# First pair with its adjacency chunks loaded ahead of x, most of its operands built on Pool, and each later pair's scale spread to all partitions by two DMAs

## The chip, the cores and the metric

The kernel runs on one core of one Trainium2 chip. The time is device microseconds of that core, the median of three runs. TensorE multiplies, VectorE and ScalarE (ACT) work on elements, Pool (GpSimd) and SyncE (SP) issue most of the transfers; SP's and ACT's transfers are generated by hardware, Pool's by software.

## The reference

```
def _L0_gnn_ref(cur, incidence_m):              # N = 4096, D = 512
    mask = incidence_m > 0
    head = mask.astype(incidence_m.dtype)
    head = head / maximum(sqrt(sum(head * head, axis=-1)), EPS)
    inc = incidence_m + head
    return (inc @ cur) / sum(inc, axis=-1)

def _L1_gnn_ref(X, A, W):
    A2 = A + eye(N)
    dscale = diagonal(A2) ** (-0.5)
    temp = A2 @ X @ W.T
    return relu((dscale[:, None] * A2 * dscale[None, :]) @ temp)

x = layernorm(x + _L0_gnn_ref(x, adj))
x = layernorm(x + _L1_gnn_ref(x, adj, W))
```

All is fp32; adj is 4096 x 4096. Each row of `inc` is adj plus, at its positive entries, one over the square root of their number. That number per row is what the text calls the scale (its reciprocal root).

## The kernel before, in words

The big products are done by a Strassen-like scheme with seven products in place of eight. Layer 0 works on 16 pairs of row blocks (rows j x 128 and (j + 16) x 128). A pair goes through four chunks; a chunk `a` holds 128 partitions by four quarters by 512 columns of the transposed adjacency, 1 MB, loaded by SP into a ring of three. For every chunk VectorE (`prepare1`)

- adds two quarters into `sr` (line 383), the raw sums that a Pool DMA (line 403) writes to `oa` in DRAM for layer 1;
- makes the mask times scale by one product for each half (393) and adds it to the chunk (395);
- forms four sums `s` (`add_up`, lines 159 to 162).

TensorE (`multiply1`, 417) then multiplies the four 128-column parts with blocks of x, seven products each, into seven PSUM banks: 28 products, 56 matmul instructions. The x side of these products needs four sums too, T1 to T4; `build` makes them once for each of the 16 blocks on VectorE (123 to 126), four instructions of 128x256. After four chunks `combine` empties the banks, and `layer0` and `operands` finish the previous pair during the next.

The scale of a pair must lie along the free dimension and be equal on all partitions. For pair 0, `count_first` takes signs of the four chunks on ACT (302), and 32 matmuls with a matrix of ones add them up over partitions and leave the total in all partitions (320). For later pairs ACT counts the signs of 16 tiles `nat` of the natural adjacency, and `spread` has three parts: reduce and root (355, 306 to 308); reciprocal and two diagonal matrices `d` (360, 363); a matmul of ones with `d` (368) and a copy out of PSUM (370). In steady state parts 0, 1 and 2 stand at chunk 2 of a pair around `prepare1` and `multiply1`; for pair 1 they stand at chunk 3 of pair 0.

The order is written out by hand: each engine takes its instructions in program order, and waits on semaphores only for what it reads or overwrites. SP issues in order, with at most eight transfers under way, each on one of eight semaphores in turn. At the start SP loads four blocks of x, three chunks and the fourth chunk (`last`, which is loaded again later), then the rest of x with five `nat` tiles in between. VectorE builds blocks 0 to 3 first, the other twelve during the chunks of pair 0.

After layer 0, layer 1's products (lines 252 and 625) fill the time from about 830 us on; nothing there is changed.

Of the kernel before, what the change touches and what calls it, by code (L numbers as in the profile page):

```python
# [8 lines left out]
F32 = mybir.dt.float32  # L9
BF16 = mybir.dt.bfloat16  # L10
AF = mybir.ActivationFunctionType
ALU = mybir.AluOpType

P = 128
LN_EPS = 1e-5
EPS = 1e-12


A12, A11, A22, A21 = range(4)

B11, B21, B22, T1, T2, T3, T4 = range(7)
# [5 lines left out]
def tile_adj_resnorm_d2(  # L27
# [37 lines left out]
    nc = tc.nc  # L65
    N, D = x.shape
    H = D // 2
    NB = N // P
    NP = NB // 2
    ND = D // P  # L70
    CK = 4
    NC = NP // CK
    CW = CK * P
    W = H + 2
# [20 lines left out]
    def spare():  # L95
        return bank(7)
# [8 lines left out]
    nc.gpsimd.memset(eps_t, LN_EPS)  # L105
    tiny = const.tile([P, 1], F32, name="tiny")
    nc.gpsimd.memset(tiny, -(2.0 ** -63))
    dscale = const.tile([P, NB], F32, name="dscale")
    nc.gpsimd.dma_start(out=dscale, in_=diag)

# [10 lines left out]
    def outer_sums(t, b11, b12, b21, b22):  # L121

        nc.vector.tensor_sub(t[:, 0, :], b11, b12)
        nc.vector.tensor_sub(t[:, 2, :], b22, b12)
        nc.vector.scalar_tensor_tensor(t[:, 1, :], t[:, 0, :], -1.0, b22, op0=ALU.mult, op1=ALU.subtract)
        nc.vector.tensor_add(t[:, 3, :], b21, t[:, 1, :])

# [139 lines left out]
    w1_pool = scope.enter_context(tc.tile_pool(name="w1", bufs=2))  # L267
    pools["turn"], pools["work"] = [ring] * 2, work

    ones_f = w1_pool.tile([P, P], F32, name="ones_f", bufs=1)  # L270
    nc.gpsimd.memset(ones_f, 1.0)
    ones_b = w1_pool.tile([P, P], BF16, name="ones_b", bufs=1)
    nc.gpsimd.memset(ones_b, 1.0)
    chunks, sums, slots, counts, scale, natural = {}, {}, {}, {}, {}, {}
    xr = {}

    def half_tile(dtype=F32, width=CW):
        return w1_pool.tile([P, 2, width], dtype, tag="u", name="u", bufs=3)

    def load_chunk(n):  # L280
        a = ring.tile([P, 4, CW], F32, tag="a", name="a")
# [2 lines left out]

    def load_x(kk):

        s = feats_pool.tile([P, 7, W], F32, name=f"b{kk}")
        lo, hi = x[kk * P:(kk + 1) * P, :], x[(kk + NP) * P:(kk + NP + 1) * P, :]
        nc.sync.dma_start(out=s[:, B11:T4 + 1:T4, 0:H], in_=split(lo))
        nc.sync.dma_start(out=s[:, B21:B22 + 1, 0:H], in_=split(hi))  # L290
        nc.gpsimd.memset(s[:, B11:B21 + 1, H:W], 1.0)
        nc.gpsimd.memset(s[:, T1, H:W], 1.0)
        slots[kk] = s

    def build(kk):

        s = slots[kk]
        outer_sums(s[:, T1:T4 + 1, 0:H], s[:, B11, 0:H], s[:, T4, 0:H], s[:, B21, 0:H], s[:, B22, 0:H])

    def signs(y, a, accum=None):  # L300

        nc.scalar.activation(y, a, AF.Sign, bias=tiny, scale=2.0 ** 64, accum_out=accum)  # L302

    def to_scale(n, total):

        nc.vector.tensor_scalar(n, total, 0.5, N / 2, op0=ALU.mult, op1=ALU.add)
        nc.vector.tensor_scalar(n, n, EPS * EPS, None, op0=ALU.max)
        nc.scalar.activation(n, n, AF.Sqrt)

    def count_first(parts):  # L310

        ps = spare()[:, 0:2 * P].rearrange("p (h i) -> p h i", h=2)
        for c, a in enumerate(parts):
            m = half_tile(BF16, 2 * CW)
            m = m.rearrange("p h (q i) -> p (h q) i", q=2)
            signs(m, a)
            for i in range(CK):
                for z in range(2):
                    first, last = c + i + z == 0, c == NC - 1 and i == CK - 1 and z == 1
                    nc.tensor.matmul(ps, ones_b, m[:, z::2, i * P:(i + 1) * P], start=first, stop=last)  # L320
        s = w1_pool.tile([P, 2, P], F32, name="sc")
        to_scale(s, ps)
        nc.vector.reciprocal(s, s)
        scale[0] = s

    tiles = iter([(j, h, t) for j in range(1, NP) for h in range(2) for t in range(NT)])
    waiting = []
# [18 lines left out]
            signs(nat, nat, counts[j][:, h, t:t + 1])  # L346
            load_natural()

    spreading = {}

    def spread(j, part):

        if part == 0:
            n = small.tile([P, 2], F32, name="n")
            nc.vector.tensor_reduce(n, counts.pop(j), axis=mybir.AxisListType.X, op=ALU.add)
            to_scale(n, n)
            spreading[j] = n
        elif part == 1:
            n = spreading.pop(j)
            nc.vector.reciprocal(n, n)  # L360
            d = w1_pool.tile([P, 2, P], F32, name="d", bufs=1)
            for h in range(2):
                nc.vector.tensor_scalar(d[:, h, :], ident, n[:, h:h + 1], None, op0=ALU.mult)
            spreading[j] = d
        else:
            d = spreading.pop(j)
            ps = spare()
            nc.tensor.matmul(ps[:, 0:2 * P], ones_f, d.rearrange("p h i -> p (h i)"), start=True, stop=True)  # L368
            s = w1_pool.tile([P, 2, P], F32, name="sc")
            nc.scalar.copy(s.rearrange("p h i -> p (h i)"), ps[:, 0:2 * P])  # L370
            scale[j] = s

    def prepare1(n, pieces=1):


        j, c = divmod(n, NC)
        a, s = chunks[n], scale[j]
        sr, *masks = (half_tile() for _ in range(3))
        sums[n] = work.tile([P, 4, CW], F32, tag="s", name="s")
        for i in range(pieces):  # L380
            w = CW // pieces
            cols = slice(i * w, (i + 1) * w)
            nc.vector.tensor_add(sr[:, :, cols], a[:, A11:A22 + 1, cols],  # L383
                                 a[:, A21, cols].unsqueeze(1).to_broadcast([P, 2, w]))
            for h in range(2):
                t = masks[h]
                y, z = t[:, :, cols], a[:, 2 * h:2 * h + 2, cols]
                if pieces == 1:
                    parts = [[v.rearrange("p q (b i) -> p (q b) i", i=P) for v in (y, z)]]
                else:  # L390
                    parts = [[v[:, q, :].rearrange("p (b i) -> p b i", i=P) for v in (y, z)] for q in range(2)]
                for m, v in parts:
                    nc.vector.scalar_tensor_tensor(m, v, 0.0, s[:, h, :].unsqueeze(1).to_broadcast(list(v.shape)),  # L393
                                                   op0=ALU.is_gt, op1=ALU.mult)
                nc.vector.tensor_add(a[:, 2 * h:2 * h + 2, cols], a[:, 2 * h:2 * h + 2, cols], t[:, :, cols])  # L395
            add_up(sums[n][:, :, cols], a[:, :, cols])
        if j // CK == c:
            add_identity(sr[:, :, (j % CK) * P:(j % CK + 1) * P])

        q = ((A11, A12), (A21, A22))[j // NQ][c * CK // NQ]  # L400
        i0 = j % SB * P
        dst = outer_1[j % NQ // SB][c % (NQ // CK), :, :, q, i0:i0 + P].rearrange("k p i -> p k i")
        nc.gpsimd.dma_start(out=dst, in_=sr.rearrange("p m (k i) -> p (m k) i", i=P))  # L403

    def multiply1(n, acc):
        c = n % NC
# [58 lines left out]
        nc.gpsimd.dma_start(out=in_outer(2, j, slice(T1, T4 + 1)), in_=t)  # L465


    for kk in range(CK):
        load_x(kk)
    for n in range(3):  # L470
        load_chunk(n)
    last = work.tile([P, 4, CW], F32, tag="s", name="s")
    nc.sync.dma_start(out=last, in_=adj_q[0, NC - 1])
    for kk in range(CK, NP):
        load_x(kk)
        if kk >= 2 * CK and len(waiting) < 5:
            load_natural()
    for kk in range(CK):
        build(kk)
    count_first([chunks[0], chunks[1], chunks[2], last])  # L480
    prepare1(0, pieces=CK)

    C = None
    for n in range(NP * NC):
        j, c = divmod(n, NC)
        if c == 0:
            if j > 0:
                C = combine(acc)
            acc = [bank(m) for m in range(7)]
        if n + 2 >= NP * NC:  # L490
            load_up_to(n + 2 - NP * NC)
        elif n > 0:
            load_chunk(n + 2)
        if j == 0 and c < NC - 1:
            for kk in range((c + 1) * CK, (c + 2) * CK):
                build(kk)
        if j + 1 < NP and c == (3 if j == 0 else 2):
            spread(j + 1, 0)
            if j == 0:
                spread(1, 1)  # L500
                spread(1, 2)
        if n + 1 < NP * NC:
            prepare1(n + 1)
        else:
            prepare(0)
        if 0 < j < NP - 1 and c == 2:
            spread(j + 1, 1)
        multiply1(n, acc)
        if 0 < j < NP - 1 and c == 2:
            spread(j + 1, 2)  # L510
        count(((5, 5, 6, 4) if j == 0 else (6, 6, 0, 4))[c])
        if j == 1 and c == 1:
            nc.vector.tensor_scalar(dscale, dscale, 1.0, None, op0=ALU.add)
            nc.scalar.activation(dscale, dscale, AF.Sqrt)
            nc.vector.reciprocal(dscale, dscale)
        if j > 0 and c == 1:
            layer0(j - 1, C)
        if j > 0 and c == 2:
            operands(j - 1, C)
        if c == 3:  # L520
            load_rows(j)
# [291 lines left out]
```

## Time and profile before

| | |
|---|---|
| median of 3 runs | 2347.87 us (2345.51 to 2349.18) |
| the profiled execution | 2345.41 us |
| its span | 2343.6 us |
| TensorE busy | 2277.4 us, 97% |
| VectorE busy | 1832.7 us, 78% |
| ACT, Pool busy | 351.5 and 220.7 us |
| moved by DMA | 552.97 MB, 236 GB/s on average |
| first product of pair 0 | at 28.10 us |

The profile is of one execution. Its page gives busy times, a chain of work followed back from the end, and groups of instructions by line; the trace behind it answers by stretch of time or by engine. "Idle before, releaser" is the time an engine stood still ahead of an instruction, and what it waited for. Matmul instructions are counted singly: an fp32 product is two of them.

### The profile page before, as it was taken

What the parts mean: (1) busy time and instruction counts of PE and PEld (TensorE: products, weight loads), DVE (VectorE), ACT (ScalarE), POOL (GpSimd) and SP (SyncE); (2) the same over time, 40 slices, a digit from 0 to 9 for tenths busy, and PEclk for the clock granted to TensorE, in tenths of its full rate; (3) what the DMA queues carried; (4) which work ended last, traced back from release to release, by engine and by line L of the source; (5) the groups of instructions that cost most, each with busy time, mean ns of one, the idle gap of its engine ahead of it and who ended that gap; (6) DMA issues with size and microseconds to landing.
All of it is one profiled execution on the core that took longest, in us unless ns stands there. A gap on an engine that the chain in (4) does not pass through costs nothing.

```text
span 2343.6 us, 21028 instructions
## 1 busy us (share of the span) xinstructions
PE 2277.4 (97%) x7166; PEld 1352.6 (58%) x7166; DVE 1832.7 (78%) x2727; ACT 351.5 (15%) x806; POOL 220.7 (9%) x372
## 2 busy tenths in 40 slices
PE   4999999999999999999999999999999999999996
PEld 3788888888888844444444444444444444444443
DVE  6898888888889857888666779766567798767796
ACT  3232333323333000000000000000000011200013
POOL 0011111111111110000001100011100000000010
PEclk8999999999999999999999999999999999999998
DMA  9577777777776466575566757567666576765672
GB/s 318 197 252 252 262 244 253 258 255 260 251 256 235 172 261 242 207 276 204 202 252 229 274 186 267 186 237 286 225 238 223 214 253 237 267 231 216 224 260 77
DMA packets 148011, 552.97 MB, mean 236 GB/s; under 512 B 15920, under 2 KB 24128, under 8 KB 108864
## 3 DMA queue, kind: packets, MB, share of 16 engines
q1 hardware_dynamic: 114192, 418.42, 51.0%
q0 software_dynamic: 33712, 133.21, 14.9%
q8 instruction: 57, 0.93, 0.2%
q14 instruction: 50, 0.41, 0.0%
HBM read 438.32 MB, written 113.25 MB: 235 GB/s over the span
## 4 chain that ended last, share of the span: by engine, by line
PE 86%; DVE 8%; issue 3%; DMA 2%; ACT 0%; POOL 0%; SPq 0%; ACTq 0%; DVEq 0%; POOLq 0%
PE q L252 55%; PE q L417 26%; PE q L625 5%; DVE a L395 1%; DVE u L393 1%; DVE s L159 1%; DMA a<-oa 1%; DVE u L383 1%; DMA s<-adj_q 1%; DVE s L161 1%; PE q L645 1%; DMA oa<-u 0%; DVE c L553 0%; DVE s L162 0%; PE q L368 0%
## 5 line engine op out<-in xcount | busy, mean ns | idle before, releaser
L252 PE MATMUL q<-s,ts 128*128 128x512 f32 x1344 | 616.0, 594 | 1.0 <-DVE u L544 1.0
L417 PE MATMUL q<-b,s 128*128 128x256 f32 (+1 forms) x2048 | 488.5, 381 | 2.3 <-DVE s L161 2.3
L159 DVE TENSOR_TENSOR s<-a 128x1024 f32<-128x1024 f32 (+1 forms) x243 | 294.1, 1210 | 203.5 <-PE q L252 173.8
L252 PEld LDWEIGHTS q<-s,ts 128*128 128x128 f32 x1344 | 256.2, 191 | 325.7 <-issue 296.6
L417 PEld LDWEIGHTS q<-b,s 128*128 128x128 f32 x2048 | 389.8, 190 | 61.0 <-DVE s L161 3.7
L417 PE MATMUL q<-b,a 128*128 128x258 f32 (+1 forms) x1536 | 381.8, 383 | 10.1 <-issue 10.1
L252 PE MATMUL q<-a,tr 128*128 128x512 f32 x704 | 333.5, 596 | 5.1 <-DMA tr<-ob 4.2
L417 PEld LDWEIGHTS q<-b,a 128*128 128x128 f32 x1536 | 293.9, 192 | 52.9 <-issue 10.7
L252 PE MATMUL q<-s,tr 128*128 128x512 f32 x448 | 228.8, 592 | 0.0
L252 PEld LDWEIGHTS q<-a,tr 128*128 128x128 f32 x704 | 132.1, 191 | 162.1 <-issue 158.1
L302 ACT ACTIVATE nat<-nat,tiny 128x512 f32<-128x512 f32 x240 | 171.0, 715 | 208.2 <-DMA nat<-adj 208.1
L252 PE MATMUL q<-a,ts 128*128 128x512 f32 x352 | 180.2, 593 | 3.1 <-DVE c L549 2.9
L393 DVE SCALAR_TENSOR_TENSOR u<-a,sc 128x1024 f32<-128x1024 f32 (+1 forms) x142 | 157.6, 1114 | 24.8 <-ACT sc L370 14.4
L161 DVE TENSOR_TENSOR s<-a,s 128x512 f32<-128x512 f32 (+1 forms) x243 | 166.5, 685 | 8.3
L162 DVE TENSOR_TENSOR s<-a,s 128x512 f32<-128x512 f32 (+1 forms) x243 | 166.5, 685 | 8.3
L395 DVE TENSOR_TENSOR a<-a,u 128x1024 f32<-128x1024 f32 (+1 forms) x134 | 157.7, 1177 | 6.8
L252 PEld LDWEIGHTS q<-s,tr 128*128 128x128 f32 x448 | 85.1, 190 | 107.3 <-issue 99.0
L542 ACT COPY p<-q 128x512 f32<-128x512 f32 x28 | 16.4, 585 | 754.9 <-PE q L252 754.9
L252 PEld LDWEIGHTS q<-a,ts 128*128 128x128 f32 x352 | 66.5, 190 | 88.7 <-issue 77.0
L625 PE MATMUL q<-wt,c 128*128 128x512 f32 x256 | 115.1, 592 | 0.0
L159 DVE TENSOR_TENSOR s<-r 128x1024 f32<-128x1024 f32 x48 | 58.7, 1223 | 70.1 <-PE q L252 65.0
L403 POOL DMA_DIRECT2D oa<-u x64 | 57.6, 901 | 465.8 <-DVE u L383 211.2
(121 smaller groups left out, 1581.2 us busy)
## 6 DMA issues: line engine op xcount, KB each, us to landing
a<-adj_r SPq DMA_DIRECT2D x112, 1024.0 KB, 6.1
a<-oa SPq DMA_DIRECT2D x80, 1024.0 KB, 5.3
a<-adj_q SPq DMA_DIRECT2D x64, 1024.0 KB, 6.1
nat<-adj SPq DMA_DIRECT2D x240, 256.0 KB, 6.9
tr<-ob SPq DMA_DIRECT2D x112, 512.0 KB, 3.7
oa<-u POOLq DMA_DIRECT2D x64, 512.0 KB, 7.9
oa<-r POOLq DMA_DIRECT2D x32, 1024.0 KB, 6.6
y<-x POOLq DMA_DIRECT2D x64, 256.0 KB, 6.1
```

The source lines that it names most:

```text
L159: nc.vector.tensor_add(s[:, S3:S1 + 1, :], a[:, A11:A22 + 1, :], a[:, A21, :].unsqueeze(1).to_broadcast([P, 2, w]))
L161: nc.vector.tensor_add(s[:, S2, :], a[:, A11, :], s[:, S1, :])
L162: nc.vector.tensor_add(s[:, S4, :], a[:, A12, :], s[:, S2, :])
L252: nc.tensor.matmul(acc[m], left, right, start=(kk == 0), stop=(kk == NQ - 1))
L302: nc.scalar.activation(y, a, AF.Sign, bias=tiny, scale=2.0 ** 64, accum_out=accum)
L383: nc.vector.tensor_add(sr[:, :, cols], a[:, A11:A22 + 1, cols], a[:, A21, cols].unsqueeze(1).to_broadcast([P, 2, w]))
L393: nc.vector.scalar_tensor_tensor(m, v, 0.0, s[:, h, :].unsqueeze(1).to_broadcast(list(v.shape)), op0=ALU.is_gt, op1=ALU.mult)
L395: nc.vector.tensor_add(a[:, 2 * h:2 * h + 2, cols], a[:, 2 * h:2 * h + 2, cols], t[:, :, cols])
L403: nc.gpsimd.dma_start(out=dst, in_=sr.rearrange("p m (k i) -> p (m k) i", i=P))
L417: nc.tensor.matmul(acc[m][:, 0:w], left, b[:, right, 0:w], start=(kk == 0), stop=(kk == NP - 1))
L625: nc.tensor.matmul(pv, C_of[2][h][f][:, 2 * r + e, cols], wt[:, 2 * f + e, :], start=(f + e == 0), stop=(f + e == 2))
L645: nc.tensor.transpose(ps[:, at + i * P:at + (i + 1) * P], C_of[3][h][d // 2][:, 2 * r + d % 2, cols], ident)
```

## The change

The diff has three parts.

- Order of the start: the four chunks of pair 0 are loaded ahead of x, and counted in halves as they land. The signs go into the places of blocks 12 to 15 of x, which are not loaded yet. The raw sums of chunks 0 and 1 (`raw_sums`, split from `prepare1`) are made early. A first Sqrt on a 128x1 tile stands ahead of all signs.
- Operands: `build` has another form (one 128x512 instruction and three of 128x256), and takes an engine: Pool for blocks 4 to 15, VectorE for 0 to 3, which stand between parts of chunk 0's work. Pool's builds stand behind the raw-sum DMAs of chunks 0 and 1 and ahead of those of chunks 2 and 3.
- Scale: half the sum plus N/2 is put into ACT's Sqrt as scale and bias, and the maximum comes after it. For pairs 1 to 15 the 128x2 result goes by a DMA on ACT's queue to DRAM, and by a second to a 128x128x2 tile in all partitions; the diagonals, the matmul, the copy and `ones_f` go. The scale tile now has its two halves interleaved, so the product reads it with a step of two elements. All pairs have the same place for this, chunk 2; counts in pair 0 move from 5, 5, 6, 4 to 8, 8, 0, 4.

The shared buffers `u` (three) become `mask` (one) and `sr` (two).

```diff
+    half_n = const.tile([P, 1], F32, name="half_n")
+    nc.gpsimd.memset(half_n, N / 2)
+    nc.scalar.activation(small.tile([P, 1], F32, name="sd"), eps_t, AF.Sqrt)
...
-    def build(kk):
-        s = slots[kk]
-        outer_sums(s[:, T1:T4 + 1, 0:H], s[:, B11, 0:H], s[:, T4, 0:H], s[:, B21, 0:H], s[:, B22, 0:H])
+    def build(kk, engine):
+        s = slots[kk][:, :, 0:H]
+        engine.tensor_sub(s[:, T1:T3 + 1:2, :], s[:, B11:B22 + 1:2, :],
+                          s[:, T4, :].unsqueeze(1).to_broadcast([P, 2, H]))
+        engine.tensor_sub(s[:, T2, :], s[:, T4, :], s[:, B11, :])
+        engine.tensor_sub(s[:, T2, :], s[:, T2, :], s[:, B22, :])
+        engine.tensor_add(s[:, T4, :], s[:, B21, :], s[:, T2, :])
...
     def to_scale(n, total):
-        nc.vector.tensor_scalar(n, total, 0.5, N / 2, op0=ALU.mult, op1=ALU.add)
-        nc.vector.tensor_scalar(n, n, EPS * EPS, None, op0=ALU.max)
-        nc.scalar.activation(n, n, AF.Sqrt)
+        nc.scalar.activation(n, total, AF.Sqrt, bias=half_n, scale=0.5)
...
     def spread(j, part):
         if part == 0:
...
-        elif part == 1:
-            n = spreading.pop(j)
-            nc.vector.reciprocal(n, n)
-            d = w1_pool.tile([P, 2, P], F32, name="d", bufs=1)
-            for h in range(2):
-                nc.vector.tensor_scalar(d[:, h, :], ident, n[:, h:h + 1], None, op0=ALU.mult)
-            spreading[j] = d
-        else:
-            d = spreading.pop(j)
-            ps = spare()
-            nc.tensor.matmul(ps[:, 0:2 * P], ones_f, d.rearrange("p h i -> p (h i)"), start=True, stop=True)
-            s = w1_pool.tile([P, 2, P], F32, name="sc")
-            nc.scalar.copy(s.rearrange("p h i -> p (h i)"), ps[:, 0:2 * P])
-            scale[j] = s
+        else:
+            n = scale.pop(j)
+            nc.vector.tensor_scalar(n, n, EPS, None, op0=ALU.max)
+            nc.vector.reciprocal(n, n)
+            row = dram.tile([P, 2], F32, name=f"sc{j}")
+            nc.scalar.dma_start(out=row, in_=n)
+            scale[j] = w1_pool.tile([P, P, 2], F32, name="sc")
+            nc.scalar.dma_start(out=scale[j].rearrange("p i h -> p (i h)"),
+                                in_=row.rearrange("i h -> (i h)").partition_broadcast(P))
...
-    for kk in range(CK):
-        load_x(kk)
-    for n in range(3):
+    for n in range(NC - 1):
         load_chunk(n)
     last = work.tile([P, 4, CW], F32, tag="s", name="s")
     nc.sync.dma_start(out=last, in_=adj_q[0, NC - 1])
+    for c in range(NC):
+        count_first(0, c, chunks[c] if c < NC - 1 else last, ps)
+    for kk in range(2 * CK):
+        load_x(kk)
+    while len(waiting) < 5:
+        load_natural()
+    for kk in range(2 * CK, NP):
+        load_x(kk)
+    for n in range(2):
+        early.add(n)
+        raw_sums(n)
     for kk in range(CK, NP):
-        load_x(kk)
-        if kk >= 2 * CK and len(waiting) < 5:
-            load_natural()
-    for kk in range(CK):
-        build(kk)
-    count_first([chunks[0], chunks[1], chunks[2], last])
-    prepare1(0, pieces=CK)
+        build(kk, nc.gpsimd)
+    build(0, nc.vector)
+    scale[0] = w1_pool.tile([P, P, 2], F32, name="sc")
+    to_scale(scale[0], ps)
+    nc.vector.tensor_scalar(scale[0], scale[0], EPS, None, op0=ALU.max)
+    nc.vector.reciprocal(scale[0], scale[0])
+    sums[0] = work.tile([P, 4, CW], F32, tag="s", name="s")
+    to_inc(0, slice(0, P))
+    build(1, nc.vector)
+    to_inc(0, slice(P, CW))
+    build(2, nc.vector)
+    build(3, nc.vector)
...
-        if j == 0 and c < NC - 1:
-            for kk in range((c + 1) * CK, (c + 2) * CK):
-                build(kk)
...
+        scales = j < NP - 1 and c == 2
+        if scales:
             spread(j + 1, 0)
...
-            prepare1(n + 1)
+            prepare1(n + 1, between=(lambda: spread(j + 1, 1)) if scales else None)
...
-        count(((5, 5, 6, 4) if j == 0 else (6, 6, 0, 4))[c])
+        count(((8, 8, 0, 4) if j == 0 else (6, 6, 0, 4))[c])
```

In the new `prepare1` the raw sums come first (unless made early), then `between` (maximum, reciprocal and the two DMAs of the next scale), then `to_inc` (mask products, additions and `add_up`), which for chunk 0 is called with columns 0 to 127 and 128 to 511.

## The prediction

> **What bounds the kernel now.** I read the page's busy times first.
>
> ```profile
> PE 2277.4 (97%) x7166; PEld 1352.6 (58%) x7166; DVE 1832.7 (78%) x2727; ACT 351.5 (15%) x806; POOL 220.7 (9%) x372
> ```
>
> TensorE is idle for only 66 us of 2343.6, so a gain must either remove TensorE work or fill idle time. Next, the answer by stages says where the idle time is (columns: stretch, its length, busy PE, PEld, DVE, ACT, POOL with counts, granted clock, DMA share, GB/s).
>
> ```profile
> 0.00:28.00 28.00, 5.80 (x32) 3.83 (x32) 9.57 (x24) 10.77 (x7) 2.94 (x43) 0.99 0.94 336
> 28.00:45.00 17.00, 15.39 (x56) 12.57 (x56) 16.24 (x52) 5.93 (x15) 0.91 (x1) 0.82 1.08 374
> 45.00:60.00 15.00, 8.41 (x23) 6.40 (x24) 14.66 (x26) 5.96 (x16) 0.89 (x1) 0.66 0.57 193
> 60.00:85.00 25.00, 19.75 (x91) 16.62 (x89) 23.93 (x40) 1.02 (x3) 1.77 (x2) 0.94 0.53 189
> ...
> 100.00:150.00 50.00, 50.00 (x232) 43.73 (x231) 44.68 (x70) 16.34 (x46) 7.85 (x11) 1.00 0.71 244
> ```
>
> Up to 85 us VectorE is nearly full (14.66 of 15, 23.93 of 25) while TensorE waits; from 100 us on TensorE is full and VectorE has some 5 us in 50 to spare. The waiting is in TensorE's own order of time (start, duration, line, what it writes and reads, then the idle time before it):
>
> ```profile
> 42.90 0.59 PE L417 MATMUL q<-b,a 128*128 128x256 f32 x2
> 49.32 2.06 PE L417 MATMUL q<-b,a 128*128 128x258 f32 x4 [5.82 <-issue]
> 53.65 3.79 PE L417 MATMUL q<-b,s 128*128 128x256 f32 x8 [2.27 <-DVE s L161]
> ...
> 85.02 1.22 PE L368 MATMUL q<-d,ones_f 128*128 128x256 f32 x2 [5.27 <-DVE d L363]
> ```
>
> The last fence is the chain of work that ended last. A pair is 224 matmul instructions in 48.53 us, so a chunk (56) takes 12.13, and the broadcast matmul L368 stands in the chain once a pair.
>
> ```profile
> 86.24 49.88 PE q L417 x224
> 136.12 0.43 PE q L368 x2
> 136.55 48.53 PE q L417 x224
> 185.09 0.43 PE q L368 x2
> ```
>
> The first pair's last chunk starts at 86.24, so the first chunk of pair 1 ends at 86.24 + 2 x 12.13 = 110.5. From there TensorE runs full. This is my reference point: what it moves by, the end moves by. The page's chain agrees: L417 26% and L252 55% of it are TensorE.
>
> **What the Trainium skill says.** (1) SBUF — State Buffer, "Who interferes with whom": a VectorE instruction with two SBUF inputs contends with a GpSimd instruction that reads SBUF; "the other fully blocks". The trace of before has no such overlap: after 4 us Pool only issues DMAs. (2) GPSIMD Engine Reference, "3.1 Elementwise — side-by-side cycle accounting": an fp32 two-input add of 2048 elements takes 4497 ns on GpSimd at about 2.6 cycles an element. Scaled, 512 elements are about 1.17 us and 256 about 0.62; estimates from that page, with no row here beside them (VectorE's 256-wide ones take 0.42). (3) SBUF — State Buffer, "Door 1", on 16-byte lines: two hits a line keep full rate. The scale is now read with a step of 8 bytes, just inside; no row of before has such a step.
>
> **The change part by part.**
>
> *Steady state, pairs 1 to 15.* L368 leaves TensorE: 0.43 us a pair. For 14 pairs (the one in the first pair is part of the head below) 14 x 0.43 = 6.0 us of pure gain, as TensorE is full there. VectorE loses L306, L307 and two L363 (0.17 + 0.17 + 0.48) and gains a maximum (0.17): 0.65 us lighter, from about 44.3 to 43.7 of 48.5. In place of the matmul, ACT issues a store of 1 KB and, when that has landed, a load to 128 partitions. Behind these on ACT are four counting activations; the copies that empty PSUM come some 24 us later, so they are covered. VectorE's sums of the raw chunk precede the maximum, so the scale is asked for at about 222.3 in the frame of the third pair (L383 at 220.88 plus 1.14 and two small ones) and first used at about 232.5 (L383 at 231.72, plus 1.14, less what is dropped): 10.2 us. Two issues near 0.6 us and two landings: the nearest rows are 2.6 us (dscale, idle queues) and 3.0 (128 KB to ob), and 6.9 under load (nat). So 6 to 15 us, and I take 8: nothing to wait for. A late scale first eats the spare 4.8 us of VectorE; only above 15 us does TensorE wait. SP and Pool keep their steady streams.
>
> *Head, order of transfers.* Chunks go first: 4.2 MB, at the 390 to 438 GB/s the trace shows between 8 and 20 us and some start-up, are in by about 13.2 (before 20.48). The first signs, in halves, end near 15.3 (128x2048 takes 1.99); four matmuls 0.5, Sqrt 0.42 and the hops 16.5. The dropped table load (1.28) was covered by transfers, so I count nothing. On VectorE build(0) must wait for x (16.0) and takes 1.85 (0.72 + 0.34 + 0.36 + 0.43), then maximum 0.29 and reciprocal 1.75, then the first product and add: first lefts at 20.7, where before TensorE began at 28.10. x follows at 1.42 us a pair of blocks (512 KB at 370 GB/s), so the fifth is in at 21.7 and the last at about 43. SP's issues (0.55 to 0.65 each) keep pace.
>
> *Head, who builds.* VectorE's remaining work to the sums of pair 1's first chunk: chunk 0 in two parts 2.8 (27.14 to 29.97 in the chain) and 5.7 (widths 384 and 768 between the 0.42, 0.69 and 1.22 rows), builds 1 to 3 5.5, chunk 1 without raw sums 7.5 (208.8 to 216.3), chunks 2, 3 and 4 8.6 + 8.6 + 9.0, small ones 0.6: 48.3 us. Pool: 12 blocks of (1.17 + 3 x 0.62) = 36.4 us.
>
> If the port is shared by turns, each of Pool's 48 instructions waits for one of VectorE's. Those 48 turns of VectorE, from the second half of chunk 0's first part to chunk 3, come to about 36 us, so Pool is done at 21.7 + 36.4 + 36 = 94. Block 15 is needed before that only near the end: pair 0's products end at 104.8 (chunk 3's sums are ready at about 93, then its 12 us). Behind Pool's builds stand its DMA issues for the raw sums of chunks 2 and 3. Their buffers are two, so chunk 4's raw sums wait for the landing of chunk 2's: 94 + 0.9 issue + 5 (3.5 to 7.9 by rows) = 100; raw sums to 101.2, products and S2 to 108.8, the rest of that chunk on TensorE 10.8: 119.6. Against 110.5 that is +9.1. Blocked Pool instructions start late, which the same skill section gives as about 115 ns after the end of VectorE's; 48 of them are 5.5, of which I let 2 lie on the path.
>
> Sum: +9.1 + 2 - 6.0 = +5.1 us. Against the profiled execution's own 2345.41 (span 2343.6 and 1.8 around it) this is 2350.5; that execution is 2.46 below the median of 2347.87, so 2353.0 for the median.
>
> **Bounds of what isn't in the trace.** Pool's prices: with 0.9 and 0.5 us the same working gives 110 to 114 for the reference point, with 1.3 and 0.72 it gives 123 to 127, so -4 to +12 in all. The step of 8 bytes: from nothing to a doubling of eight 1.14 us products a pair, +9.1, which is 4.3 over VectorE's spare time, or +64 over 15 pairs. Restarts of TensorE after gaps (clock 0.5 to 0.8 in the first 90 us of before) come in both kernels; +-2.
>
> **Rivals.**
> (a) *No contention* (0.16), the other side: Pool does 3.0 us a block against TensorE's 3.03, done by 58. TensorE runs from 20.7 with stalls of 1.7 + 2.3 + 1.9 (first chunk in two parts, chunk 1's sums), pair 0 ends near 76, raw sums of chunk 4 are not late, and the reference point is 88 to 90: -21 - 6.0 = -27, 2321. For it: everything else in the head is shorter by this order. Against: the skill's section. The span between the two cases is 121.6 - 88 = 33.6 us, and the kernel breaks even at a reference point of 116.5: so it is faster as soon as less than 85% of the blocked time remains.
> (b) *Shared access by access* (0.13): the VectorE instructions stretch by less than a full turn, some 10 us earlier, 2343.
> (c) *The scale is late* (0.11): DMA round trip over 15 us, or the stepped read costing; each us over the spare is paid 15 times; +15 to +64, 2363 to 2412. Against: the light store and load, and two hits a line.
> The likeliest, turns on the port, has 0.60; its own range is 2343 to 2363.
>
> **How the numbers follow.** 0.2% is 4.7 us, about what can be told from no change. Turns: slower 0.38, same 0.15, faster 0.07. (a): faster 0.16. (b): faster 0.11, same 0.02. (c): slower 0.10, same 0.01. Together faster 0.34, same 0.18, slower 0.48. The range reaches down over (a) with its 2 to 4 us of uncertainty and up to the start of (c): 2317 to 2365, with little more than 0.1 outside.
>
> **What would show it.** Turns: VectorE's 128x1024 products near 1.9 us instead of 1.22 and Pool's 256-wide sums over 1 us between 22 and 94 us; Pool's first raw-sums issue after the builds near 94; TensorE waits on Pool's or VectorE's lines up to 105. If Pool is done by 60 and products stay at 1.22, (a) holds. In the steady part pairs of 48.5 us with no L368 and no wait on the scale tile confirm the 6 us; VectorE waits on the scale over 4 us, or products longer there, show (c). A head whose first matmul comes well after 22 would mean that my landing times fail.

## The result

| | before | after |
|---|---|---|
| median, 12 runs each | 2347.82 us (2345.19 to 2351.42) | 2355.37 us (2350.24 to 2367.00) |
| ratio to before | | 1.0034, 95% interval 1.0021 to 1.0047 |
| profiled execution, its span | 2345.41, 2343.6 us | 2359.78, 2358.0 us |
| first product of pair 0 | 28.10 us | 20.67 us |

The kernel is 7.5 us slower by medians. The profiled execution of after is 4.4 us above its median and that of before 2.4 below its own, so the two spans differ by 14.4 us; what follows accounts for that 14.4, and sets medians beside the sizes where there are any.

The page's busy times of after:

```profile
PE 2281.7 (97%) x7136; PEld 1348.8 (57%) x7136; DVE 1836.7 (78%) x2612; ACT 348.1 (15%) x795; POOL 285.0 (12%) x420
```

Pool has gained 64 us, and VectorE hasn't lost any: 115 instructions fewer, but 4 us more. By stages (same columns as in the prediction: busy PE, PEld, DVE, ACT, POOL, clock, DMA share, GB/s):

```profile
0.00:28.00 28.00, 14.41 (x46) 8.72 (x46) 14.91 (x22) 10.71 (x11) 11.40 (x52) 1.00 0.98 350
45.00:60.00 15.00, 7.40 (x24) 5.09 (x23) 14.72 (x11) 7.68 (x22) 14.53 (x12) 0.72 0.84 279
60.00:85.00 25.00, 24.39 (x109) 20.85 (x107) 24.38 (x18) 3.23 (x9) 24.45 (x16) 0.97 0.24 57
85.00:100.00 15.00, 11.86 (x53) 10.16 (x54) 5.55 (x7) 4.28 (x12) 5.29 (x7) 0.97 0.73 248
```

Two things are new. From 45 to 85 us Pool is full beside VectorE. From 85 to 100 us VectorE works only 5.55 of 15 us. TensorE's order of time names the waits (start, duration, line, operands, count, then the idle time before it):

```profile
96.07 0.59 PE L415 MATMUL q<-b,a 128*128 128x256 f32 x2
99.64 1.20 PE L415 MATMUL q<-b,a 128*128 128x258 f32 x2 [2.98 <-ACT nat L309]
105.39 1.20 PE L415 MATMUL q<-b,a 128*128 128x258 f32 x2 [4.55 <-DVE deg L426]
...
305.64 1.20 PE L415 MATMUL q<-b,a 128*128 128x258 f32 x2 [3.86 <-DVE deg L426]
```

Pair 0 ends early (its last product is at 96 us), but the first chunk of pair 1 then stalls, and TensorE stalls again in the steady part, at 305.64, where before had nothing of this size. (The wait ahead of 99.64 is put down to ACT. VectorE's addition L392, which makes the operand, ends at 99.54 in its own order of time, so it is probably VectorE's.) The chain of work that ended last (start, length, what) says what was late both times:

```profile
86.59 8.78 DMA oa<-sr
95.39 1.24 DVE sr L371
...
278.39 11.02 DMA sc<-n
289.43 7.78 DMA sc<-sc
297.24 1.24 DVE mask L390
...
305.64 50.07 PE q L415 x218
```

At 86.59 it is Pool's transfer of pair 0's raw sums; at 278.39 the store and the load of a scale. `deg`, which TensorE waits for, is the second instruction of `combine` (L426). It stands on VectorE behind `prepare1` of the next pair's first chunk; a late scale delays that `prepare1`, hence `combine`, hence the emptying of the banks that the next pair's products need. The waits from 86 to 850 us, first VectorE's for the scale, then TensorE's for `deg` (us in total, times, longest):

```profile
DVE mask L390 <- DMA sc<-sc: 55.9, 14, 8.5
```

```profile
PE q L415 <- DVE deg L426: 11.7, 7, 4.5
```

For bookkeeping I use one mark, the start of ACT's first copy `p` in `combine`, in each pair: it starts as soon as TensorE has finished a pair's first bank. Pair 1's stands at 146.12 us in before and at 153.18 in after; pair 15's at 832.05 and 844.73. So 7.1 us are lost by pair 1, another 5.6 from pair 1 to pair 15 (691.55 against 685.93), and 1.7 after that, where nothing was changed. The 1.7 says little: from the last mark to the end, the executions of this study took anything from 1509.6 to 1517.5 us.

### The profile page after: what moved, and what is told of

It reads as the page before. It is cut to its first block, busy times and chain, and to the rows that moved or that the text cites. A ratio compares the mean times of both kernels' runs of the same rounds, so it can differ in the third digit from the quotient of the medians.

```text
span 2358.0 us, 20987 instructions
## 1 busy us (share of the span) xinstructions
PE 2281.7 (97%) x7136; PEld 1348.8 (57%) x7136; DVE 1836.7 (78%) x2612; ACT 348.1 (15%) x795; POOL 285.0 (12%) x420
## 4 chain that ended last, share of the span: by engine, by line
PE 75%; DVE 13%; DMA 8%; POOL 2%; issue 2%; ACT 1%; SPq 0%; DVEq 0%; ACTq 0%; POOLq 0%
PE q L259 53%; PE q L415 17%; PE q L632 5%; DMA sc<-n 3%; DVE a L392 2%; DVE mask L390 2%; DVE s L166 2%; DMA sc<-sc 1%; DMA b<-x 1%; DVE s L168 1%; DVE sr L371 1%; DMA a<-oa 1%; DMA nat<-adj 1%; DMA a<-adj_r 1%; POOL b L301 1%
## 5 line engine op out<-in xcount | busy, mean ns | idle before, releaser
L415 PE MATMUL q<-b,s 128*128 128x256 f32 (+1 forms) x2048 | 493.7, 384 | 11.2 <-DVE s L168 10.5
L390 DVE SCALAR_TENSOR_TENSOR mask<-a,sc 128x1024 f32<-128x1024 f32 (+2 forms) x134 | 161.8, 1210 | 58.2 <-DMA sc<-sc 55.9
L392 DVE TENSOR_TENSOR a<-a,mask 128x1024 f32<-128x1024 f32 (+2 forms) x130 | 161.8, 1244 | 6.6
L378 POOL DMA_DIRECT2D oa<-sr x64 | 57.8, 903 | 348.7 <-DVE sr L371 237.0
```

What stands on the lines that cost most here:

```text
L390: nc.vector.scalar_tensor_tensor(m, v, 0.0, s[:, :, h].unsqueeze(1).to_broadcast(list(v.shape)), op0=ALU.is_gt, op1=ALU.mult)
L392: nc.vector.tensor_add(z, z, y)
L415: nc.tensor.matmul(acc[m][:, 0:w], left, b[:, right, 0:w], start=(kk == 0), stop=(kk == NP - 1))
```

## The experiments

All medians stand beside runs of before on the same chip, whose medians were 2347.99, 2347.54 and 2348.61 us. "Marks" are the copies `p` of pairs 0, 1 and 15, and "steady" is the last minus the middle one. Each row of marks is from one profiled execution. The landing time of a transfer runs from its issue to its completion.

| kernel | median us | ratio to before, 95% | marks of pairs 0, 1, 15 | steady |
|---|---|---|---|---|
| before | 2347.8 | | 97.16, 146.12, 832.05 | 685.93 |
| after | 2355.4 | 1.0034 (1.0021 to 1.0047) | 94.10, 153.18, 844.73 | 691.55 |
| 1 after, matmul scale | 2349.1 | 1.0008 (1.0000 to 1.0017) | 99.27, 148.26, 833.39 | 685.13 |
| 2 before, DMA scale | 2356.1 | 1.0039 (1.0026 to 1.0052) | 92.69, 141.23, 840.95 | 699.72 |
| 3 after, builds on VectorE | 2340.4 | 0.9968 (0.9959 to 0.9977) | 93.20, 141.73, 824.05 | 682.32 |
| 4 after, Pool fills | 2328.2, one run | | 75.62, 129.37, 808.92 | 679.55 |
| 5 after, raw sums on ACT | 2341.1 | 0.9980 (0.9967 to 0.9993) | 93.92, 142.46, 825.32 | 682.86 |
| 6 before, unused stores | 2347.3, one run | | 98.13, 147.10, 832.93 | 685.83 |
| 7 before, early DMA scale | 2336.1 | 0.9948 (0.9936 to 0.9961) | 92.53, 141.07, 820.59 | 679.52 |
| 8 after, VectorE, early | 2337.2 | 0.9951 (0.9937 to 0.9964) | 93.33, 141.87, 821.39 | 679.52 |
| 9 after, ACT, early | 2337.9 | 0.9955 (0.9941 to 0.9968) | 93.97, 142.50, 822.02 | 679.52 |
| 10 after, early | 2347.2 | 0.9994 (0.9985 to 1.0002) | 93.97, 153.36, 832.88 | 679.52 |
| 11 before, stores at two moments | 2388.9, one run | | 97.92, 152.48, 874.14 | 721.66 |

The steady part at its best is 679.5 us, fourteen distances of about 48.53. Against that, before loses 6.4 us (the matmul in 13 pairs, and 0.8 once between pairs 4 and 5) and after 12.0.

**1. After with the scale by matmul.** Does the start lose the time, or the scale's two DMAs?

```diff
-            row = dram.tile([P, 2], F32, name=f"sc{j}")
-            nc.scalar.dma_start(out=row, in_=n)
-            scale[j] = w1_pool.tile([P, P, 2], F32, name="sc")
-            nc.scalar.dma_start(out=scale[j].rearrange("p i h -> p (i h)"),
-                                in_=row.rearrange("i h -> (i h)").partition_broadcast(P))
+            for h in range(2):
+                nc.vector.tensor_scalar(d[:, h, :], ident, n[:, h:h + 1], None, op0=ALU.mult)
...
+            nc.tensor.matmul(ps[:, 0:2 * P], ones_f, d.rearrange("p h i -> p (h i)"), start=True, stop=True)
+            s = w1_pool.tile([P, P, 2], F32, name="sc")
+            nc.scalar.copy(s.rearrange("p i h -> p h i"), ps[:, 0:2 * P].rearrange("p (h i) -> p h i", h=2))
```

> The changed kernel with the scale spread by the matmul with ones again (parts 0 to 2 at chunk 2, for all pairs); its start is kept. My theory: the start costs +8.7 us at the end of pair 1's first chunk (119.2 against 110.5) through turns on the port, and the scale's two DMAs cost VectorE 56 us of waiting and TensorE some 7 us of stalls and as much in slower restarts, which eat the 6.0 us of the dropped matmul. So this kernel: no wait on the scale tile above 2 us, pairs of 48.96 us, and 2347.8 + 8.7 = 2356.5, +-3. Rival (the DMAs are neutral and all of the loss is the start, the 6 us having come in): +8.7 + 6 more than the changed kernel less its loss, 2361 or over. Rival (the DMAs are the main loss): 2350 or under.

2349.1 us: my expectation of 2356.5 failed, and the rival held. Nearly all of the loss goes with the DMAs. Part of it is in the start: pair 1's mark is 4.9 us earlier than in after. The raw sums' transfer made VectorE wait 4.75 us here and 9.24 in after. Steady is back at 685.1, with the matmul's 0.43 us a pair in it.

**2. Before with the scale by DMAs**, everything else as before.

```diff
-            nc.tensor.matmul(ps[:, 0:2 * P], ones_f, d.rearrange("p h i -> p (h i)"), start=True, stop=True)
...
+            nc.scalar.dma_start(out=row, in_=n)
+            scale[j] = w1_pool.tile([P, P, 2], F32, name="sc")
+            nc.scalar.dma_start(out=scale[j].rearrange("p i h -> p (i h)"),
+                                in_=row.rearrange("i h -> (i h)").partition_broadcast(P))
...
-            prepare1(n + 1)
+            prepare1(n + 1, between=(lambda: spread(j + 1, 1)) if scales else None)
```

> The kernel before with the scale part alone: two DMAs on ACT's queue at chunk 2 for all pairs, interleaved halves; its start and VectorE's builds are kept. My theory: TensorE's wait of 5.27 us ahead of the matmul of pair 0 goes (-5), the steady part gains 6.0 for the matmul and gives 4 to 10 back through VectorE's waits for the scale (about 4 us in each pair): 2343 to 2347. Rival (steady gain comes in whole, VectorE's spare time covers the wait): 2337. Rival (steady loss over 10): 2349 or over. VectorE waits for the scale in 13 or more pairs, store landing near 9.7 us.

2356.1: my expectation failed, the rival held. Pair 1's mark is 4.9 us better (the matmul's wait on `d` in pair 0 is gone), then 13.8 us more are lost in steady state than in before. VectorE's wait for the scale (86 to 850 us):

```profile
DVE u L386 <- DMA sc<-sc: 46.0, 15, 9.9
```

Not all of the 13.8 need be the scale's: VectorE also waited 19.2 us for the raw sums' transfers to free the buffers `u`, which the masks share here. In after, where `sr` has buffers of its own, such a wait occurs only in the start.

**3. After with all builds on VectorE**, four ahead of each chunk as in before.

```diff
-    for kk in range(CK, NP):
-        build(kk, nc.gpsimd)
...
+        if j == 0 and c < NC - 1:
+            for kk in range((c + 1) * CK, (c + 2) * CK):
+                build(kk, nc.vector)
```

> The changed kernel with blocks 4 to 15 built on VectorE again, four ahead of each later chunk of pair 0 as before; the order of transfers, the early raw sums and the DMAs are kept. My theory (Pool and VectorE take turns on the port, so a Pool build costs VectorE about as much as Pool's own time): the work to pair 1's first chunk on VectorE is 48.3 + 12 x 1.85 = 70.5 us from 20.7, the raw sums of chunk 4 wait for no builds, pair 1's first chunk ends near 102 (119.2 in the changed kernel): -17, so 2338. Rival (Pool's builds are nearly free and the start is lost elsewhere, as in the late landing of the raw sums): pair 1's first chunk ends at 119 or later, 2355 or more.

2340.4 (2338 expected), 15 us better than after and faster than before. Pair 0 ends only 0.9 us earlier; pair 1 follows after 48.53 us instead of 59.08. So Pool's builds do harm after pair 0, not in it.

**4. Fills in place of Pool's sums.** Twelve blocks get constants, so T1 to T4 of these blocks are left out.

```diff
-        build(kk, nc.gpsimd)
+        b = slots[kk][:, :, 0:H]
+        nc.gpsimd.memset(b[:, T1:T3 + 1:2, :], 1.0)
+        nc.gpsimd.memset(b[:, T2, :], 1.0)
+        nc.gpsimd.memset(b[:, T2, :], 1.0)
+        nc.gpsimd.memset(b[:, T4, :], 1.0)
```

> The changed kernel with Pool filling the four sums of blocks 4 to 15 with a constant, in instructions of the same sizes that read nothing; it leaves these sums out, so its products are not those of the reference. My theory (it is the reads that take the port): VectorE's 128x1024 products are 1.22 us from the start, none near 2; Pool is done soon after the last block of x lands (near 44 us); TensorE runs from 20.7 with the stalls of 1.7, 2.3 and 1.9 us, pair 1's first chunk ends at 88 to 90. Rival (contention is with any Pool instruction): products near 2 us and an end of that chunk over 95.

VectorE's order of time in after, with Pool's beside it, and then both engines here, while Pool fills:

```profile
49.23 2.17 DVE L392 TENSOR_TENSOR a<-a,mask 128x1024 f32<-128x1024 f32 x1
51.43 1.63 DVE L390 SCALAR_TENSOR_TENSOR mask<-a,sc 128x1024 f32<-128x1024 f32 x1
53.10 1.63 DVE L392 TENSOR_TENSOR a<-a,mask 128x1024 f32<-128x1024 f32 x1
```

```profile
48.07 2.25 POOL L301 TENSOR_TENSOR b<-b 128x512 f32<-128x512 f32 x1
50.28 1.70 POOL L303 TENSOR_TENSOR b<-b 128x256 f32<-128x256 f32 x1
52.06 1.59 POOL L304 TENSOR_TENSOR b<-b 128x256 f32<-128x256 f32 x1
```

```profile
34.53 1.22 DVE L390 SCALAR_TENSOR_TENSOR mask<-a,sc 128x1024 f32<-128x1024 f32 x1
35.78 1.23 DVE L392 TENSOR_TENSOR a<-a,mask 128x1024 f32<-128x1024 f32 x1
```

```profile
34.31 0.53 POOL L487 MEMSET b<- 128x512 f32 x1
34.77 0.31 POOL L488 MEMSET b<- 128x256 f32 x1
35.14 0.31 POOL L489 MEMSET b<- 128x256 f32 x1
35.57 0.31 POOL L490 MEMSET b<- 128x256 f32 x1
```

With both engines adding, they run in step, one instruction for one: Pool starts at 48.07, 50.28 and 52.06, VectorE at 49.23, 51.43 and 53.10. With Pool only writing, VectorE's instructions of this size take 1.22 or 1.23 us. (Pool's fills are also shorter than its sums, but four of them fall into these two instructions and lengthen neither.) That is what the Trainium skill says (SBUF — State Buffer, "Who interferes with whom"): a two-input VectorE instruction contends with a Pool instruction that reads, not with one that only writes. The mark of pair 0 is 18.5 us earlier than in after. Pair 1's first chunk ended at about 95 us, not at the 88 to 90 expected: VectorE waited 6.85 us for ACT's counts of pair 1, which now came last, and then 3.57 for its scale.

**5. After with two transfers of raw sums off Pool's queue.**

```diff
-        nc.gpsimd.dma_start(out=dst, in_=sr.rearrange("p m (k i) -> p (m k) i", i=P))
+        queue_of = nc.scalar if n in (2, 3) else nc.gpsimd
+        queue_of.dma_start(out=dst, in_=sr.rearrange("p m (k i) -> p (m k) i", i=P))
```

> The kernel after, but the raw-sum DMAs of pair 0's chunks 2 and 3 are issued on ACT's queue and no longer stand behind Pool's builds. If the prediction's step is right (chunk 4's raw sums wait for the landing of chunk 2's, which Pool issued only after its builds), the wait of 9.24 us ahead of raw sums (L371) goes, the first pair-to-pair distance falls from 59.1 to about 50 us, and with the steady losses unchanged the time is about 8 us less: 2347. Rival: the copies of the raw sums are not what ends that stage (the previous experiments put only about 1 us on the start); then another wait takes its place and the time stays at 2353 to 2356.

VectorE's first instruction for pair 1, in after and then here (the idle time before it in brackets, none here):

```profile
95.39 1.22 DVE L371 TENSOR_TENSOR sr<-a 128x1024 f32<-128x1024 f32 x1 [9.24 <-DMA oa<-sr]
```

```profile
85.90 1.66 DVE L371 TENSOR_TENSOR sr<-a 128x1024 f32<-128x1024 f32 x1
```

The wait is gone, the first distance is 48.54 us, and the median falls by 14.3 us, more than the 8 expected. 10.7 of it is pair 1's mark. The rest is a smaller steady loss (682.86 against 691.55, in single executions of kernels whose times scatter by 15 and 17 us): TensorE waits for `deg` twice here, and in after six times past the start. Why the scale comes late less often here I haven't shown.

**6. Three unused stores on ACT's queue**, in before. Is the store slow because its rows have 8 bytes?

```diff
+            nc.scalar.dma_start(out=probe8, in_=n)
+            nc.scalar.dma_start(out=probe_far[:, 0:2], in_=n)
+            nc.scalar.dma_start(out=probe512, in_=d[:, 0, :])
```

> The kernel before with three unused stores a pair on ACT's queue at the place of part 1: 128 rows of 8 bytes side by side (1 KB), 128 rows of 8 bytes that lie 512 bytes apart in DRAM, and 128 rows of 512 bytes (64 KB). Theory: the small store is slow because its rows are small; then the two stores of 8-byte rows land in 8 to 10 us and the 64-KB store in 5 or less. Rival: every transfer on this queue waits behind the load of the chunks; then all three have about the same landing time, and it grows with the place in the queue. Nothing but the three issues (3 x 0.33 us on ACT a pair) is added, so the time should be within 3 us of before.

The DMA list here (out<-in, queue, count, KB each, median us from issue to landing), with that of after below it:

```profile
pc<-d ACTq DMA_DIRECT2D x15, 64.0 KB, 4.5
pa<-n ACTq DMA_DIRECT2D x15, 1.0 KB, 3.2
pb<-n ACTq DMA_DIRECT2D x15, 1.0 KB, 3.8
```

```profile
sc<-sc ACTq DMA_DIRECT2D x15, 128.0 KB, 5.3
...
sc<-n ACTq DMA_DIRECT2D x15, 1.0 KB, 9.7
```

The rows are not the cause: a store of the same form lands in 3.2 us at this place (2.7 to 5.1), which is at the end of VectorE's work on the chunk, and in 9.7 in after. My theory failed; the three land close together, a little later with each place in the queue, as the rival said. The stretch in which one such store was under way, first in after (issued at 229.05, landed in 9.7), then here (issued at 428.46, landed in 3.2), in the columns of the table by stages:

```profile
229.00:239.00 10.00, 10.00 (x48) 8.71 (x47) 9.62 (x13) 0.00 (x0) 2.90 (x5) 1.00 0.94 249
```

```profile
428.46:431.66 3.20, 3.20 (x17) 2.79 (x16) 3.05 (x7) 0.00 (x0) 0.79 (x1) 1.00 0.17 40
```

The DMA engines were busy 0.94 of the time there and 0.17 here, in these two of the 15 stores each.

**7. Before with the DMA scale of experiment 2, one chunk earlier.**

```diff
-        scales = j < NP - 1 and c == 2
+        scales = j < NP - 1 and c == (2 if j == 0 else 1)
...
-        count(((8, 8, 0, 4) if j == 0 else (6, 6, 0, 4))[c])
+        count(((8, 8, 4, 4) if j == 0 else (8, 0, 4, 4))[c])
```

> The kernel before with the scale by two DMAs, asked for one chunk earlier (chunk 1 of a pair, for pair 1 at chunk 2), with the counts moved ahead to match. If the round trip's length alone made the DMA form slow (previous run: +8.1 us on before), the wait of VectorE on the scale (46 us over 15 pairs) is gone, the pairs are 48.53 us, and the time is 2337 to 2342, 6 to 10 us below before. Rival: the transfers themselves disturb VectorE or the loads, wherever they stand; then it stays above 2349.

2336.1 us, a little below the 2337 to 2342 expected and 20 below experiment 2, from which only the place and the counts differ; experiments 8 and 9 come within 2 us of it. VectorE's wait on the scale falls from 46.0 us to 0.4:

```profile
DVE u L386 <- DMA sc<-sc: 0.4, 1, 0.4
```

In the chain of work TensorE's products of layer 0 are one piece from here on, with nothing between (start, length, what, instructions):

```profile
83.56 739.54 PE q L410 x3412
```

The scale also lands somewhat sooner at this place (load 3.6 us by median, 5.3 in experiment 2; store 7.5 and 7.7). That isn't needed for the result: one chunk earlier adds 12 us to the 10.2 that the prediction found available, so that even the longest round trip of after, 18.8 us, would be in time.

The gain over before has two parts by the marks: 5.05 us at pair 1 and 6.4 in the steady part.

**8. After with builds on VectorE and the early scale.** The edits of 3 and 7 together.

> The kernel after with all builds on VectorE and the scale asked for one chunk earlier. Both losses named so far are taken away: start as in the run with VectorE's builds (2340.4) and no wait on the scale; pair 1 to pair 15 should take 679.6 us (14 pairs of 48.53) in place of 682.3 there. Expected 2337, at most 2339. Rival: the counts, which now stand in a shorter stretch (8, 0, 4, 4), or the loads of the natural tiles become the late thing; then VectorE waits on ACT's counts instead and the time is 2340 or more.

2337.2, as expected; steady is 679.52.

**9. After with ACT's transfers and the early scale**, so with Pool's builds kept; the edits of 5 and 7.

> The kernel after with both losses taken away and Pool's builds kept: raw sums of pair 0's chunks 2 and 3 issued on ACT's queue, and the scale asked for one chunk earlier. Pair 0 as in the run with ACT's issues (copies of p at about 93.9), then 48.53 us a pair without exceptions. Expected 2337. This compares Pool's builds with VectorE's (2337.2 in the run with both on VectorE): if they share the port by turns, 12 builds on Pool are worth nothing and the two agree within 2 us; rival: Pool's builds are worth the 22 us of VectorE's work that they save and only the hazards hid it; then 2330 or less.

2337.9, within 1 us of experiment 8. What Pool's twelve builds are worth can be seen by stages. First here (builds on Pool), then experiment 8 (builds on VectorE):

```profile
28.00:45.00 17.00, 8.95 (x22) 6.78 (x23) 16.72 (x15) 4.39 (x13) 16.45 (x15) 0.60 1.08 360
45.00:60.00 15.00, 7.70 (x30) 6.01 (x30) 14.72 (x11) 1.47 (x5) 14.53 (x12) 0.81 0.42 146
60.00:85.00 25.00, 24.04 (x109) 20.56 (x107) 24.34 (x19) 9.80 (x27) 24.45 (x16) 0.98 0.65 189
```

```profile
28.00:45.00 17.00, 9.24 (x40) 7.80 (x41) 16.42 (x31) 4.34 (x12) 0.00 (x0) 0.94 1.08 359
45.00:60.00 15.00, 12.60 (x46) 10.03 (x45) 14.56 (x24) 7.61 (x22) 0.89 (x1) 0.73 0.77 261
60.00:85.00 25.00, 19.27 (x80) 15.69 (x79) 24.07 (x36) 3.93 (x11) 1.70 (x2) 0.91 0.46 137
```

From 28 to 85 us VectorE does 15 + 11 + 19 = 45 instructions in one and 31 + 24 + 36 = 91 in the other, and is busy 55.8 and 55.1 us. Pair 0's marks, 93.97 and 93.33, show that it gets as far in one as in the other. The work that moved to Pool came back as longer instructions.

**10. After with the early scale alone.**

> The kernel after with the scale asked for one chunk earlier, and nothing else: Pool still issues the raw sums of chunks 2 and 3 behind its builds. The distance from pair 0 to pair 1 stays near 59 us (48.53 without the late issue), the later pairs take 48.53. Expected 2347, 8 below after, in equal parts with what the other run takes away. Rival: the two losses are one (the late start of pair 1 makes the scales late); then the later pairs still show distances of 49 to 55 us and the time is 2352 or more.

2347.2, as expected to 0.2 us. Pair 1 is as late as in after (mark at 153.36), and every later pair takes 48.53. So the late start of pair 1 alone doesn't slow the later pairs, and the losses are two: experiment 5 takes away the first, this one the second. They aren't quite independent, since in experiments 3 and 5, which take away the first, the steady loss is smaller as well.

**11. Small stores at two moments of two chunks**, in before.

```diff
+        m = small.tile([P, 2], F32, name="pv")
+        nc.vector.tensor_copy(m, pair_of)
+        nc.scalar.dma_start(out=dram.tile([P, 2], F32, name=f"{place}{'abcd'[c]}{j}"), in_=m)
```

> The kernel before with four unused stores of 128 rows of 8 bytes a pair on ACT's queue: right after the raw sums of chunks 1 and 3, and at the end of VectorE's work on these chunks, about 7 us later. The previous probes, all at the later moment, landed in 3.2 us (8-byte rows), 3.8 (far apart) and 4.5 (512-byte rows), so small rows are not what makes the store of the scale take 9.7 us in the kernel after. If it is the moment (it is asked for just when the raw sums' transfer and a chunk's load are under way), the stores after the raw sums land in 7 to 10 us and those at the end in 3 to 4. Rival: the moment doesn't matter and the store is slow because ACT's queue holds another transfer in that kernel; then all four land in 3 to 4.

The landing times of the stores made for chunk 3 (the chunk at which after asks for its scale), right after the raw sums and at the end:

```profile
DMA to landing us min/median/max: 4.4/7.9/9.7
```

```profile
DMA to landing us min/median/max: 2.9/7.5/8.9
```

For chunk 1 the medians were 4.8 and 4.3. So the moment matters, from 3 to nearly 10 us for one and the same store, with nothing large on ACT's queue; but my expectation failed, since chunk 3 was slow at both places. The end of chunk 3 is also the place of experiment 6, where the store took 3.2, so the place in the program alone doesn't decide. Is it the traffic? The DMA engines' busy share in the first 3 us after each issue goes with it here: 34 stores with a share of 0.8 or more landed in 4.4 to 9.7 us, 24 with 0.6 or less in 2.6 to 5.7. But in experiment 10 two stores of the scale landed in 3.4 and 3.7 us at shares of 1.15 and 1.23 (the view's share can pass 1). So the traffic as a cause is argued, not shown; it was not varied alone. This kernel was 40 us slower, which I had not foreseen: each store waits for VectorE in ACT's program order, and ACT's counts and roots stand behind it (ACT's `nat` waited 119.0 us in all for the probe's `pv`).

## Why the prediction was right, and where not

The time was 2.4 us from the prediction, on the side that was given the larger chance. Against before the prediction had +5.1 and the medians show +7.5. The direction was foreseen, and how the start loses time. The closeness of the number is luck, for two terms were off in opposite directions: the start lost 7.4 us and not 11.1, and the steady part lost 5.6 where 6.0 was to be gained. Had the steady part come out as predicted, the kernel would be 1.4 us slower, which can't be told from no change.

- **L368 leaves TensorE, 0.43 us a pair: right, but not collected.** Experiments 7 to 10 run at 48.53 us a pair, 6.4 us less in all than before's 685.93. In after the gain turned into a loss of 5.6 in its profiled execution, 12.0 against the best; experiment 10, which takes only the late scale away, puts its price at 8.2 us by medians.
- **"So 6 to 15 us, and I take 8: nothing to wait for": the step that failed, by its size.** The store took 9.7 us and the load 5.3 by median. In the 14 pairs in which VectorE waited, 12.4 to 18.8 us passed from the store's issue to the first product with the scale (13.9 in the middle), against 10.2 available. The rows taken as nearest were those of other moments. The Trainium skill gives about 2.0 us fixed for a transfer on Pool's path (DMA: Bandwidth & Descriptors, "Anatomy of one DMA — SWDGE (gpsimd) path"); on ACT's path, under load, the runs show a multiple of it for 1 KB.
- **"Only above 15 us does TensorE wait": right, nearly to the number.** TensorE waited for `deg` in the six of these pairs in which the scale took 14.7 us or more, for 0.25 to 3.86 us, and in none of the eight with 14.0 or less (the seventh wait is that of the start). What was put at nothing is the price of such a stall. The longest, ahead of 305.64, took 3.86 us, but its pair took 6.7 longer than 48.53. The rest is slower products: the clock granted to TensorE from 305.64 to 310 was 0.50, and the 218 instructions took 50.07 us, where at the pace of the other pairs they take 47.2.
- **Rival (c), late scale,** therefore took place beside the likeliest case, by the sign given for it, waits of VectorE over 4 us. It cost less than its range of 15 to 64, since only six pairs in 14 came past the spare time.
- **Stepped read:** free, as taken. The product of mask and scale takes 1.22 us with the interleaved tile, as with before's.
- **First lefts at 20.7:** first product at 20.67.
- **Turns on the port: right in the main** (experiments 4 and 9); the skill's section says only that such instructions contend. Pool's builds ran from 21.28 to 86.65 us, 65.4 in place of 72.4. Pool's prices, estimates from the skill's GPSIMD Engine Reference, "3.1 Elementwise — side-by-side cycle accounting", were a little low: the shortest of Pool's sums took 1.26 us (512 wide) and 0.70 (256) against 1.17 and 0.62. But in step, a product and a Pool sum of 256 have a period of 1.67 us (53.10 less 51.43), less than 1.22 + 0.70. Pool was done 7 us earlier, and pair 0 ended at 96.7, not 104.8.
- **Rivals (a) and (b):** (a) fell, since Pool was done at 86.65 and not at 58, and VectorE's products were longer. Of (b) there is a little: the turns overlap in part.
- **Chunk 4's raw sums wait for Pool's late transfer: right,** and this is what makes the start slow (experiment 5). From the start of its issue it took 8.78 us, not 5.9. In experiment 1 it took 5.1, and there four loads of `nat` came after it; in after SP had asked for them at 83.97, ahead of it; that this is the reason is argued. With `combine` late, and 4.55 us of stall for it, the reference point came to 119.3 us: pair 1's mark at 153.18 less 33.8, which is the distance in before (146.12 less 111.86, see the next point) without the 0.43 of L368. The prediction had 119.6, and 2 for late starts of Pool, which no run shows apart.
- **The reference point of before** is 111.9 and not 110.5: in the chain, 136.12 less two chunks of 12.13 us. The forward sum missed that the 224 products from 86.24 took 49.88 us. So the start lost 7.4 us, not the 11.1 predicted.
- **Where the time is:** predicted +11.1 and -6.0; found +7.1 by pair 1, +5.6 to pair 15, +1.7 after it.

Left open: what exactly delays the store, and why the scale came late in more pairs of after than of experiments 3 and 5. The 13.8 of experiment 2 aren't the scale's alone, as said there.

## What to carry to other kernels

Moving sums to Pool gave nothing here, where VectorE was the bound and both read two operands (55.8 against 55.1 us busy): count such instructions as VectorE's own until a trace shows otherwise, and see what stands behind them in Pool's queue, since a transfer issued there inherits their delay. A broadcast through DRAM that takes a matmul's place must be asked for by its longest round trip and not by a median from another moment; here one chunk (12 us) earlier turned a loss of 8 us into a gain of 11 over before (experiments 2 and 7). A stall costs more than its length if the products behind it run slower for a while, here 6.7 us for 3.86. When one instruction is late, follow what stands behind it on its own engine to the next engine: the wait that showed on TensorE was for an instruction eight places behind the late one on VectorE.

## What I had not expected of the hardware

- One store of 1 KB, 128 rows of 8 bytes, landed anywhere from 2.6 to 11.4 us in these kernels, depending on when; 64 KB beside it in experiment 6 took 4.5 by median.
- Two-input VectorE and Pool instructions in step take a little less than the shortest of each together (1.67 against 1.22 + 0.70 us), yet over 57 us the saving for VectorE was nil.
- The kernels in which VectorE waits for the scale scatter more from run to run: by 17 us in twelve runs of after and by 15, 8 and 8 in experiments 5, 2 and 3, against 3 to 6 in before and experiments 7 to 10 (five to thirteen runs each). Why wasn't tested.
